# A four-layer graph network on one core: one edge tile a group of layer 3 made on chip by TensorE instead of gathered, and another mix of gathers, single rows and TensorE in layer 2

## The chip, the core and the metric

The kernel runs on one core of a Trainium2 chip. The core has TensorE (PE: matmuls; PEld are its weight loads), VectorE (DVE), ScalarE (ACT), GpSimd (POOL) and SyncE (SP), each with its own queue of instructions. The metric is the device time of one execution in microseconds. The kernel before took 16186.58 us, the median of three runs (16184.84 to 16187.52).

## The reference

There are 12500 nodes with 64 features, 400000 edges sorted by `dst`, an edge type (8 of them) for each edge and a node type (4) for each node. Four layers follow each other, each `x = layernorm(x + layer(x))`. The change touches the third and the fourth, which the kernel and this text count from zero as layers 2 and 3:

```python
# layer 2
msg_sum = segment_sum(feature[src], dst)          # mean over the edges of each node, then
h = where(deg > 0, msg_sum / max(deg, 1), 0)      # a gate of 3 groups and a 64x64 matrix
# layer 3
k, q, v = (typed_linear(x, W, ntype) for W in (Wk, Wq, Wv))   # the matrix is chosen by node type
kw = typed_head_linear(k[src], rel_att, etype)    # 4 heads of 16, the matrix chosen by edge type
m  = typed_head_linear(v[src], rel_msg, etype)
a  = (kw * q[dst]).sum(-1) * rel_pri[:, etype].T / sqrt(16)
alpha = softmax of a over the edges of each dst
h  = segment_sum(m * alpha, dst)                  # then typed_linear(h, Wa, ntype)
```

So layer 2 needs one row of x for each edge, and layer 3 a row of 64 keys and 64 values for each edge, which depends on the source node, its type and the type of the edge.

## The kernel before, in words

**Tiling.** The edges lie in 128 lanes of `EP` = 3125 columns; a column is a tile of 128 edges. Columns are taken in groups of `G` = 25: `groups` (L194) has 124 of these, then 16, 8 and 1 columns, 127 in all. The nodes are 98 tiles of 128 (`NT`), in blocks of `NB` = 7 (`NBA` = 14). Since edges are sorted by `dst`, sums over the edges of a node are scans along a lane, and their ends are picked up later.

**Gathers.** `gather` (L214) is an indirect DMA that POOL issues: 128 rows of a table in device memory, by a column of indices, into one tile of SBUF. Instead of it, `row_by_row` (L234 on) moves single rows by direct DMAs from the queues of SP and ACT, 128 (or half of them) for one tile.

**Layer 2's edges** (L1168 to L1302) loop over the groups. Each tile `gx[:, j]` of a group comes in one of three ways: by `gather` from `X2`; in the groups of `single`, chosen by `ROWS2` (L45: those with g % 5 in (1, 3)), the last two columns by rows, one on SP and one on ACT; and in the groups of `dense` (3 to 123) `PE2` tiles (L46: 2 and 3 by turns) by TensorE. For these, `one_hots_of` spreads the keys by a matmul into `pk` (L1241) and compares them on DVE (L1244) to a one-hot tile `hot`; `products` multiplies it with x, which lies in SBUF as a sum of three bf16 `parts` (39 matmuls, L1257); of the eight nodes that share a key, `take` picks the right one by a mask and a sum on DVE (L1267 to L1270). Then 25 scans on DVE add up the rows along the lanes (L1293). The order on SP, ACT, PE and DVE is that of the program (`manual_schedule`); one-hots are made three groups ahead, products and rows two groups ahead.

**Layer 2's nodes** (`nodes2`) finish x for a block, write it to `xs`, and put into the table `TKM` in device memory keys and values for each node and each of the eight edge types. `in_turn` (L179) interleaves the stages of several blocks, in program order.

**Layer 3's edges** (L1429 to L1558): `step(g, c0, ng)` does one group. POOL gathers its 25 tiles of 128 keys and values from `TKM` (in every third group, `ROWS3`, SP loads one by rows, in two halves). DVE carries the query of each edge along the lane into `st` (25 dependent instructions, L1462), multiplies with the keys and reduces (`pr`, `sc`, five columns at a time, L1469 and L1470), scans the running maximum `M` (L1477) and takes the differences `ex`. ACT exponentiates them twice (`weight`, L1485, into PSUM; `ex`, L1486). DVE scans the sum `L` (L1489), ACT spreads the decay `dec` (L1492), DVE multiplies values by `weight` (`wm`, L1497, four instructions) and scans `hs` (L1502); ACT copies `hs`, `M` and `L` to `R` (L1505 to L1507), which SP writes out. `gk` and `st` have three buffers, so that POOL and the loads run ahead. Here only SP is in program order; the order of the other engines is a scheduler's.

**Layer 3's nodes** (`nodes3`) pick up the ends of the lanes, apply `Wa` by node type, add `xs` and normalize.

Of the kernel before, what the change touches and what calls it, by code (L numbers as in the profile page):

```python
# [19 lines left out]
P = 128  # L20
# [21 lines left out]
WAIT2 = 16  # L42
WAIT3, EVERY3 = 2, 1
ACTN = 3
ROWS2 = 5, (1, 3)  # L45
PE2 = 2, 3  # L46
NC = 13
ROWS3 = 3
RL = 32
# [5 lines left out]
def resnorm_gnn_kernel(ctx: ExitStack, tc: tile.TileContext, a: dict, out: bass.AP):  # L55
# [20 lines left out]
    NBA = NT // NB  # L76

    const = ctx.enter_context(tc.tile_pool(name="const", bufs=1))
    to_l2 = ExitStack()
    to_l0 = ExitStack()  # L80
    right = "right"
# [20 lines left out]
    def lanes(table):  # L102
        return table[:E, :].rearrange("(p c) f -> p c f", p=P)
# [110 lines left out]
    def gather(to, table, at):  # L214
        return nc.gpsimd.indirect_dma_start(  # L215
            out=to, out_offset=None, in_=table, in_offset=bass.IndirectOffsetOnAxis(ap=at, axis=0)
        )
# [168 lines left out]
    xs = const.tile([P, NT, D], F32, name="xs")  # L386
    if NREM:
        nc.vector.memset(xs[:, NFULL:, :], 0.0)
        nc.sync.dma_start(xs[:NREM, NFULL, :], x[NFULL * P :, :])
# [477 lines left out]
        nc.vector.tensor_add(fixS, pos, away)  # L867

    keep = const.tile([P, EP], F32, name="keep")
    negm = const.tile([P, EP], F32, name="negm")  # L870
    w64 = const.tile([D, P], F32, name="w64")
    neg64 = const.tile([D, P], F32, name="neg64")
    fixG = const.tile([P, 1], I32, name="fixG")
# [291 lines left out]
        in_turn(nodes01, [NB] * (NBA - 1) + [4, 2, 1], lambda n: EVERY1)  # L1165
    to_n1.close()


    with tc.tile_pool(name="e2", bufs=2) as sb:
        pm = sb.tile([P, D], F32, name="m2", bufs=1)  # L1170
# [23 lines left out]

        parts = [sb.tile([P, NT, D], BF, name=f"part{k}", bufs=1) for k in range(3)]
        for b in range(NBA):
            t = slice(b * NB, (b + 1) * NB)
            rest = xs[:, t, :]
            for k in range(3):
                nc.scalar.activation(parts[k][:, t, :], rest, AF.Copy)  # L1200
                if k < 2:
                    left = sb.tile([P, NB, D], F32, name=f"left{k}")
                    nc.vector.tensor_sub(left, rest, parts[k][:, t, :])
                    rest = left
# [5 lines left out]

        def by_pe(g):

            return range(G - 2 - PE2[g % 2], G - 2) if g in dense else ()

        keys = sb.tile([P, n], HF, name="keys", bufs=1)
        key_b = sb.tile([P, n], F32, name="key_b", bufs=1)
# [87 lines left out]
        put_ends(R2, row)  # L1304

    to_l2.close()

    def types_of(t, t0, nt):

# [23 lines left out]
    with tc.tile_pool(name="n2", bufs=1) as sb, tc.tile_pool(name="n2ps", bufs=2, space=PSUM) as psp:  # L1333
        puts = []

        def nodes2(b, t0, nt):
# [65 lines left out]
            for j in range(nt):  # L1402

                put = start_row(t0 + j, q[:, j, :])
                tc.declare_no_dep(put.ins, group="starts", reason="distinct rows")
                tc.add_to_no_dep_group("starts", put.ins)
                puts.append(put)
                s = slice(j * P, (j + 1) * P)
                km = sb.tile([P, ETY, 2, D], F32, name=f"km_{j % 4}")
                pws = [psp.tile([P, ETY, D], F32, name="pw", bufs=4) for _ in range(2)]  # L1410
                for w, pw in enumerate(pws):
                    of = slice(w * D, (w + 1) * D)
                    nc.tensor.matmul(pw.rearrange("p e f -> p (e f)"), kv[of, s], wkm[of].rearrange("p e f -> p (e f)"),
                                     start=True, stop=True)
                for w, pw in enumerate(pws):
                    nc.scalar.activation(km[:, :, w, :], pw, AF.Copy)
                r = (t0 + j) * P
                nc.sync.dma_start(
                    TKM[r * ETY : (r + P) * ETY, :].rearrange("(p e) f -> p (e f)", e=ETY),
                    km.rearrange("p e w f -> p (e w f)"),  # L1420
                )
                yield

        in_turn(nodes2, [1, 2, 4] + [NB] * (NBA - 1), lambda n: n + 1,
                {getattr(mybir.EngineType, e) for e in ('PE', 'Activation', 'DVE', 'SP')})


    with tc.tile_pool(name="e3", bufs=2) as sb, tc.tile_pool(name="e3ps", bufs=1, space=PSUM) as psp:
# [26 lines left out]
        def step(g, c0, ng):  # L1455
            nonlocal pa, M, L, hs, last, R
            gk, st = keys_of(g), sts.pop(g)
            for j in range(ng - (g in single)):
                gather(gk[:, j, :], TKM, stS[:, c0 + j : c0 + j + 1])
            for j in range(ng):  # L1460
                c = c0 + j
                nc.vector.scalar_tensor_tensor(st[:, j, :], pa, keep[:, c : c + 1], st[:, j, :],  # L1462
                                               op0=ALU.mult, op1=ALU.add)
                pa = st[:, j, :]
            sc = sb.tile([P, NH, ng], F32, name="sc")
            for q in range(0, ng, 5):
                s = slice(q, min(q + 5, ng))
                pr = sb.tile([P, 5, D], F32, name="pr")[:, : s.stop - q]
                nc.vector.tensor_mul(pr, st[:, s], gk[:, s, :D])  # L1469
                nc.vector.tensor_reduce(sc[:, :, s].rearrange("p h c -> p c h"),  # L1470
                                        pr.rearrange("p c (h d) -> p c h d", d=HS), AX.X, ALU.add)
            nm = negm[:, c0 : c0 + ng]
# [9 lines left out]
            nc.vector.tensor_sub(ex[:, 1, :, 1:], sc, M[:, :, 1:])  # L1482

            weight = psp.tile([P, NH, ng], F32, name="weight", bufs=2)
            nc.scalar.activation(weight, ex[:, 1, :, 1:], AF.Exp)  # L1485
# [27 lines left out]
            for ahead, half in ((3, 0), (2, 1)):  # L1513
                if g + ahead in single:
                    to, k = keys_of(g + ahead)[:, G - 1, :], single.index(g + ahead)
                    for p in range(half * P // 2, (half + 1) * P // 2, RL):
                        row_by_row(TKMb, 8 * D, p, (nc.sync, SP, to, places3[k : k + 1, :]))

        R = None
        with tc.manual_schedule(engines={SP}):  # L1520
            load_starts(0)
            load_starts(1)
            for g, (c0, ng) in enumerate(groups):
                step(g, c0, ng)

        row = ends_of_lanes(sb, R3, W3)

# [41 lines left out]
    with tc.tile_pool(name="n3", bufs=1) as sb, tc.tile_pool(name="n3ps", bufs=2, space=PSUM) as psp:  # L1569
        def nodes3(b, t0, nt):  # L1570
# [69 lines left out]
```

## Time and profile before

| | us |
|---|---|
| median of three runs | 16186.58 |
| profiled execution | 16233.31 |
| its span | 16231.3 |
| layer 2's edges, from the first gather on | 8385 to 11882 |
| layer 2's nodes | 11882 to 12168 |
| layer 3's edges | 12168 to 16074 |
| layer 3's nodes | 16074 to 16231 |

| engine | busy us | share of the span |
|---|---|---|
| PE | 7861.8 | 48% |
| DVE | 10882.3 | 67% |
| ACT | 2682.9 | 17% |
| POOL | 12159.1 | 75% |

The granted PE clock was 0.71 over the span. A row of the profile names the source line, the engine, the operation, the tile that is written and those that are read, the shape and the number of instructions; then their busy time, the mean of one, and how long the engine stood idle just before them and what ended that. A row of waits has the engine, what waited, what it waited for, and the total, number and longest of these waits. "issue" is time in which the engine waited for nothing that the profile shows.

### The profile page before, as it was taken

The page shows a single profiled execution, that of the slowest core. Times are in us where ns is not written, and L with a number is a line of the kernel's source. Part 1 is how long each engine was busy: PE and PEld are TensorE (multiplying, and loading weights), DVE is VectorE, ACT ScalarE, POOL GpSimd, SP SyncE. Part 2 cuts the span into 40 slices and gives each one's busy share as a digit, 9 for nine tenths or more (in the row PEclk, how much of TensorE's full clock was granted, in tenths as well). Part 3 has the DMA queues.
Part 4 walks back from the last instruction along what each step waited for, and adds up shares of the span by engine and source line. Part 5 has one row for each costly group of instructions (what it writes and reads, how often), then busy time and mean ns, then how long its engine had stood idle before and what let it go on. Part 6 is the DMA issues. An engine that isn't in the chain of part 4 may idle for free. (4 is left out here: it accounts for less than half of the span.)

```text
span 16231.3 us, 220160 instructions
## 1 busy us (share of the span) xinstructions
PE 7861.8 (48%) x54548; PEld 5552.5 (34%) x54548; DVE 10882.3 (67%) x29577; ACT 2682.9 (17%) x5002; POOL 12159.1 (75%) x12630
## 2 busy tenths in 40 slices
PE   4454666666663566666547777777760000000002
PEld 4443555555553455555523333333340000000002
DVE  9995777777774577777445555555545666666666
ACT  0012333333332011111020000000031212222222
POOL 7777777777777777777767777777767777777776
PEclk6666777777776787777768888888885555555555
DMA  3333332222221565656312222222253333333333
GB/s 78 120 104 85 87 91 82 72 56 52 53 57 48 169 201 195 204 197 202 111 41 54 59 58 57 55 58 58 58 187 103 110 108 109 113 107 111 109 109 97
DMA packets 1136527, 1634.07 MB, mean 101 GB/s; under 512 B 762674, under 2 KB 768306, under 8 KB 1134850
## 3 DMA queue, kind: packets, MB, share of 16 engines
q1 hardware_dynamic: 693282, 1094.42, 20.1%
q0 software_dynamic: 403872, 517.47, 13.6%
q10 hardware_dynamic: 38080, 8.06, 0.2%
q8 instruction: 432, 7.08, 0.2%
q14 instruction: 861, 7.05, 0.1%
HBM read 881.78 MB, written 737.15 MB: 100 GB/s over the span
## 5 line engine op out<-in xcount | busy, mean ns | idle before, releaser
L780 POOL DMA_INDIRECT SRT<-at,to x3090 | 3011.7, 975 | 943.2 <-issue 909.6
L215 POOL DMA_INDIRECT gk<-TKM,stS x3084 | 2934.3, 951 | 940.9 <-issue 926.3
L215 POOL DMA_INDIRECT gx<-X,srcS x2724 | 2591.8, 951 | 923.2 <-issue 785.3
L1257 PE MATMUL pr<-part,hot 128*128 128x512 bf16 (+1 forms) x11817 | 2549.3, 379 | 504.3 <-DVE one L1269 493.7
L215 POOL DMA_INDIRECT gb<-TB,srcS x2125 | 2079.7, 979 | 648.2 <-issue 629.0
L956 PE MATMUL ps_c<-ident,full 128*64 128x128 f32 x3 | 1.3, 421 | 3908.4 <-DVE full L1529 3906.9
L1293 DVE SCALAR_TENSOR_TENSOR gx<-gx,keep 128x64 f32<-128x64 f32 x3124 | 890.5, 285 | 1457.8 <-DMA gx<-X 1042.6
L1257 PEld LDWEIGHTS <-hot 128*128 128x128 bf16 x11817 | 1154.6, 100 | 1891.8 <-issue 674.2
L1089 DVE SCALAR_TENSOR_TENSOR R<-R,negm,msg 128x64 f32<-128x64 f32 x3124 | 854.3, 273 | 828.2 <-PE msg L1020 823.7
L956 PEld LDWEIGHTS ps_c<-ident,full 128*64 128x64 f32 x3 | 0.4, 128 | 3909.8 <-DVE full L1529 3907.7
L215 POOL DMA_INDIRECT xg<-in_x,srcS x1000 | 956.0, 956 | 306.3 <-issue 297.6
L1469 DVE TENSOR_TENSOR pr<-st,gk 128x320 f32<-128x320 f32 x627 | 306.8, 489 | 1143.6 <-DMA gk<-TKM,stS 1117.7
L1462 DVE SCALAR_TENSOR_TENSOR st<-st,keep 128x64 f32<-128x64 f32 x3124 | 886.3, 284 | 209.0 <-DMA st<-S 114.3
L372 DVE TENSOR_TENSOR ol<-iota,lo 128x512 f16<-128x512 f32 (+2 forms) x1000 | 979.4, 979 | 0.0
L681 PE MATMUL pT<-identh,oh 128*98 128x128 f16 x3125 | 405.0, 259 | 1157.1 <-DVE oh L369 1154.8
L1014 PE MATMUL pt<-ident,st 128*128 128x128 f32 (+1 forms) x3250 | 825.7, 353 | 214.4 <-DVE st L1080 195.8
L729 PE MATMUL pG<-ol,mb 128*128 128x128 f16 x4625 | 774.1, 241 | 184.7 <-ACT mb L713 182.7
L1080 DVE SCALAR_TENSOR_TENSOR st<-st,keep 128x64 f32<-128x64 f32 x3124 | 862.3, 276 | 1.3
L1013 PE MATMUL pt<-ident,gb 128*128 128x128 f32 (+1 forms) x2210 | 574.8, 355 | 591.6 <-DMA gb<-TB,srcS 585.2
L1048 DVE SCALAR_TENSOR_TENSOR r<-r,keep 128x64 f32<-128x64 f32 x3000 | 829.9, 277 | 0.0
L369 DVE TENSOR_TENSOR oh<-iota,hi 128x392 f16<-128x392 f32 (+2 forms) x1000 | 784.6, 785 | 23.6 <-DMA xg<-in_x,srcS 23.6
L1014 PEld LDWEIGHTS pt<-ident,st 128*128 128x128 f32 (+1 forms) x3250 | 630.9, 244 | 289.1 <-DVE st L1080 243.3
(353 smaller groups left out, 19603.5 us busy)
## 6 DMA issues: line engine op xcount, KB each, us to landing
st<-S SPq DMA_DIRECT2D x248, 800.0 KB
R<-R SPq DMA_DIRECT2D x124, 900.0 KB
r<-SRT SPq DMA_DIRECT2D x125, 812.5 KB
R<-r SPq DMA_DIRECT2D x125, 812.5 KB
gx<-X ACTq DMA_DIRECT2D x6272, 0.2 KB
gx<-X SPq DMA_DIRECT2D x6272, 0.2 KB
S<-zero SPq DMA_DIRECT2D x200, 500.0 KB
R<-R SPq DMA_DIRECT2D x124, 800.0 KB
```

The source lines that it names most:

```text
L215: return nc.gpsimd.indirect_dma_start(out=to, out_offset=None, in_=table, in_offset=bass.IndirectOffsetOnAxis(ap=at, axis=0))
L369: nc.vector.tensor_tensor(oh, iota[:, None, :NT].to_broadcast([P, n, NT]), hi[:, :, None].to_broadcast([P, n, NT]), ALU.is_equal)
L372: nc.vector.tensor_tensor(ol, iota[:, None, :].to_broadcast([P, n, P]), lo[:, :, None].to_broadcast([P, n, P]), ALU.is_equal)
L729: nc.tensor.matmul(pG[:, j, :], l, r, start=(n == 0), stop=(n == len(terms) - 1))
L780: put = nc.gpsimd.indirect_dma_start(out=SRT, out_offset=bass.IndirectOffsetOnAxis(ap=to[:, j : j + 1], axis=0), in_=at[:, j, :], in_offse ...
L1014: nc.tensor.matmul(pt[:w, k, :], two_tiles(st, k, w), ident, start=False, stop=True)
L1048: nc.vector.scalar_tensor_tensor(r1[:, j, :D], pm1, keep1[:, c : c + 1], r1[:, j, :D], op0=ALU.mult, op1=ALU.add)
L1080: nc.vector.scalar_tensor_tensor(st[:, j, :], pa, keep[:, c : c + 1], st[:, j, :], op0=ALU.mult, op1=ALU.add)
L1089: nc.vector.scalar_tensor_tensor(R[:, j, :], pm, negm[:, c : c + 1], msg[:, j - q, :], op0=ALU.add, op1=ALU.max)
L1257: nc.tensor.matmul(pr[:, :m, :].rearrange("p b f -> p (b f)"), hot[:, c, :], parts[part][:, 8 * c : 8 * c + m, :].rearrange("p b f -> p (b ...
L1293: nc.vector.scalar_tensor_tensor(gx[:, j, :], pm, keep[:, c : c + 1], gx[:, j, :], op0=ALU.mult, op1=ALU.add)
L1462: nc.vector.scalar_tensor_tensor(st[:, j, :], pa, keep[:, c : c + 1], st[:, j, :], op0=ALU.mult, op1=ALU.add)
```

## The change

In layer 2, `ROWS2` becomes every third group with one residue (40 groups of two row tiles where there were 49), and `PE2` a cycle of 3, 3, 3, 2 (332 tiles by TensorE where there were 303).

In layer 3, in the 121 groups of `dense` (3 to 123), column 22 is no longer gathered. TensorE makes it from x, which `nodes2` now also leaves in SBUF as three bf16 parts `x3`, in stages that stand by hand in the steps of the groups around it. They pick the row of x (one-hot, 39 products, a mask, eight summing matmuls to `x1`) and the type of the node (13 narrow products to `p8`), multiply by the matrices of all types (`keys_and_values`), choose the edge type by a mask and sum 16 matmuls to `kv1`, and ACT puts that into `gk`. The two `weights` tiles, `p8`, `x1` and `kv1` are slices of one tile `bank2` in PSUM; `weight` was a tile of its own before. DVE, PE, ACT and SP now all keep the order of the program in this loop. `nm` is computed for each group instead of read from `negm`, `xs` and `negm` move to other pools, and `nodes3` adds the three parts of `x3` instead of `xs`.

```diff
-ROWS2 = 5, (1, 3)
-PE2 = 2, 3
+ROWS2 = 3, (1,)
+PE2 = 3, 3, 3, 2
...
+            in_parts(lambda shape, name: tile_of(shape, name, 1), xs, x3, cols)
...
+        bank = psp.tile([P, 4 * P], F32, name="bank")
+        pk, tT, kvT = bank[:, :P], bank[:, P : 3 * P], bank[:, 3 * P :]
+        bank2 = psp.tile([P, 4 * P], F32, name="bank2")
+        weights = [bank2[:, k * P : k * P + NH * G].rearrange("p (h c) -> p h c", h=NH) for k in range(2)]
+        p8 = bank2[:, 2 * P : 2 * P + 8]
+        x1, kv1 = bank2[:, 5 * D : 6 * D], bank2[:, 6 * D :]
...
+        def only(rows, hot8):
+            one = sb.tile([P, 8, D], F32, name="one", bufs=3)
+            nc.vector.tensor_mul(one, rows, hot8[:, :, None].to_broadcast([P, 8, D]))
+            return one
+        def sum_of(to, one):
+            for b in range(8):
+                nc.tensor.matmul(to, ident, one[:, b, :], start=(b == 0), stop=(b == 7))
...
+        def products_3(g):
+            hot = hots.pop(g)
+            of_x[g] = pr = psp.tile([P, 8, D], F32, name="big", bufs=2)
...
+            for c in range(NC):
+                m = min(8, NT - 8 * c)
+                nc.tensor.matmul(p8[:, :m], hot[:, c, :], ntab[:, 8 * c : 8 * c + m], start=(c == 0), stop=(c == NC - 1))
+        def take_3(g):
...
+            nc.vector.tensor_scalar(hb, frow[:, :8], key_b[:, 0, k : k + 1], None, op0=ALU.is_equal)
+            sum_of(x1, only(pr, hb))
...
+            nc.vector.tensor_mul(t8, p8, hb)
...
+        def keys_and_values(g):
...
+                pw = psp.tile([P, ETY, D], F32, name="big", bufs=2)
...
+        def choose_3(g):
...
+            chosen[g] = [only(pw, he) for pw in by_edge_type.pop(g)]
+        def sums_3(g):
+            for w, one in enumerate(chosen.pop(g)):
+                sum_of(kv1[:, w * D : (w + 1) * D], one)
+        def put_3(g):
+            nc.scalar.activation(keys_of(g)[:, by_pe, :], kv1, AF.Copy)
...
             for j in range(ng - (g in single)):
+                if g in dense and j == by_pe:
+                    continue
                 gather(gk[:, j, :], TKM, stS[:, c0 + j : c0 + j + 1])
...
                 pa = st[:, j, :]
+            on(g + 1, choose_3)
+            on(g + 3, one_hot_3)
+            on(g + 2, products_3)
+            on(g + 1, sums_3)
             sc = sb.tile([P, NH, ng], F32, name="sc")
...
-            weight = psp.tile([P, NH, ng], F32, name="weight", bufs=2)
+            weight = weights[g % 2][:, :, :ng]
             nc.scalar.activation(weight, ex[:, 1, :, 1:], AF.Exp)
             nc.scalar.activation(ex, ex, AF.Exp)
+            on(g + 3, compare_3)
...
+            on(g + 2, take_3)
             hs = sb.tile([P, D, ng + 1], F32, name="hs")
...
+            on(g + 2, place_3)
             R = sb.tile([P, ng, W3], F32, name="R", bufs=2)
...
+            on(g + 1, put_3)
             nc.sync.dma_start(lanes(R3)[:, c0 : c0 + ng, :], R)
...
-        with tc.manual_schedule(engines={SP}):
+        with tc.manual_schedule(engines={SP, ACT, mybir.EngineType.PE, mybir.EngineType.DVE}):
...
             for g, (c0, ng) in enumerate(groups):
+                on(g + 1, keys_and_values)
                 step(g, c0, ng)
...
-            nc.vector.tensor_add(y, po, xs[:, cols, :])
+            nc.vector.tensor_add(y, x3[0][:, cols, :], x3[1][:, cols, :])
+            nc.vector.tensor_add(y, y, x3[2][:, cols, :])
+            nc.vector.tensor_add(y, y, po)
```

`one_hot_3` and `compare_3` are the two halves of layer 2's `one_hots_of` for one tile. `on(g, ...)` runs the stages for group g if it is one of `dense`.

More of the change, by code (lines that the diff above doesn't have):

```diff
@@ L78, in resnorm_gnn_kernel @@
     const = ctx.enter_context(tc.tile_pool(name="const", bufs=1))
+    to_l3 = ExitStack()
+    xpool = to_l3.enter_context(tc.tile_pool(name="xpool", bufs=1))
     to_l2 = ExitStack()
@@ L384, in row_bcast @@
         return t
-    xs = const.tile([P, NT, D], F32, name="xs")
+    xs = xpool.tile([P, NT, D], F32, name="xs")
     if NREM:
@@ L869, in resnorm_gnn_kernel @@
     keep = const.tile([P, EP], F32, name="keep")
-    negm = const.tile([P, EP], F32, name="negm")
+    negm = edges2.tile([P, EP], F32, name="negm")
     w64 = const.tile([D, P], F32, name="w64")
@@ L1166, in resnorm_gnn_kernel, with in_parts @@
     to_n1.close()
+    def in_parts(tile_of, table, parts, t):
+        rest = table[:, t, :]
+        for k in range(3):
+            nc.scalar.activation(parts[k][:, t, :], rest, AF.Copy)
+            if k < 2:
+                left = tile_of([P, t.stop - t.start, D], f"left{k}")
+                nc.vector.tensor_sub(left, rest, parts[k][:, t, :])
+                rest = left
     with tc.tile_pool(name="e2", bufs=2) as sb:
@@ L1196, in resnorm_gnn_kernel @@
         for b in range(NBA):
[L1197 to L1204, printed above, removed]
+            in_parts(lambda shape, name: sb.tile(shape, F32, name=name), xs, parts, slice(b * NB, (b + 1) * NB))
         own = sb.tile([P, NC], F32, name="own", bufs=1)
@@ L1211, in by_pe @@
         def by_pe(g):
-            return range(G - 2 - PE2[g % 2], G - 2) if g in dense else ()
+            return range(G - 2 - PE2[g % len(PE2)], G - 2) if g in dense else ()
         keys = sb.tile([P, n], HF, name="keys", bufs=1)
@@ L1306, in resnorm_gnn_kernel @@
     to_l2.close()
+    parts3 = ctx.enter_context(tc.tile_pool(name="parts3", bufs=1, side=right))
+    x3 = [parts3.tile([P, NT, D], BF, name=f"x3_{k}") for k in range(3)]
+    ntab = parts3.tile([P, NT], BF, name="ntab")
     def types_of(t, t0, nt):
@@ L1422, in nodes2, with one_hot_3, compare_3, place_3 @@
                 yield
+            in_parts(lambda shape, name: tile_of(shape, name, 1), xs, x3, cols)
         in_turn(nodes2, [1, 2, 4] + [NB] * (NBA - 1), lambda n: n + 1,
                 {getattr(mybir.EngineType, e) for e in ('PE', 'Activation', 'DVE', 'SP')})
-    with tc.tile_pool(name="e3", bufs=2) as sb, tc.tile_pool(name="e3ps", bufs=1, space=PSUM) as psp:
+    to_l3.close()
+    with tc.tile_pool(name="e3", bufs=2) as sb:
+      with (tc.tile_pool(name="e3k", bufs=1) as ksb):
+        types = ksb.tile([P, NT], I32, name="types")
+        nc.vector.memset(types, 0)
+        of = a["node_type_4"]
+        nc.sync.dma_start(types[:, :NFULL], of[: NFULL * P].rearrange("(t p) -> p t", p=P))
+        if NREM:
+            nc.sync.dma_start(types[:NREM, NFULL:], of[NFULL * P :].rearrange("(t p) -> p t", t=1))
+        nc.vector.tensor_copy(ntab, types)
+        dense = range(3, NG - 1)
+        nd = len(dense)
+        by_pe = G - 3
+        keys = sb.tile([P, nd], HF, name="keys", bufs=1)
+        key_b = sb.tile([P, 2, nd], F32, name="key_b", bufs=1)
+        at = groups[dense[0]][0] + by_pe
+        of = stS[:, at : at + (nd - 1) * G + 1 : G]
+        part_i = ksb.tile([P, 4, nd], I32, name="part_i")
+        for k, (by, mask) in enumerate(((13, None), (3, 127), (10, 7), (0, 7))):
+            if by:
+                nc.vector.tensor_scalar(part_i[:, k], of, by, None, op0=ALU.arith_shift_right)
+            if mask:
+                nc.vector.tensor_scalar(part_i[:, k], part_i[:, k] if by else of, mask, None, op0=ALU.bitwise_and)
+        nc.vector.scalar_tensor_tensor(keys, part_i[:, 0], float(P), part_i[:, 1], op0=ALU.mult, op1=ALU.add)
+        nc.vector.tensor_copy(key_b, part_i[:, 2:])
+        own = sb.tile([P, NC], F32, name="own", bufs=1)
+        nc.vector.tensor_scalar(own, frow[:, :NC], float(P), pcol, op0=ALU.mult, op1=ALU.add)
+      with tc.tile_pool(name="e3ps", bufs=1, space=PSUM) as psp:
+        bank = psp.tile([P, 4 * P], F32, name="bank")
[4 more added lines that the diff above has]
+        x1, kv1 = bank2[:, 5 * D : 6 * D], bank2[:, 6 * D :]
+        hots, of_x, by_types, chosen, place_of_type, by_edge_type = {}, {}, {}, {}, {}, {}
+        def only(rows, hot8):
[5 more added lines that the diff above has]
+                nc.tensor.matmul(to, ident, one[:, b, :], start=(b == 0), stop=(b == 7))
+        def one_hot_3(g):
+            k = g - dense[0]
+            nc.tensor.matmul(pk, keys[:, k : k + 1].to_broadcast([P, P]), identh, start=True, stop=True)
+        def compare_3(g):
+            hots[g] = hot = sb.tile([P, NC, P], BF, name="hot", bufs=2)
+            nc.vector.tensor_tensor(hot, pk[:, None, :].to_broadcast([P, NC, P]),
+                                    own[:, :, None].to_broadcast([P, NC, P]), ALU.is_equal)
+        def products_3(g):
[3 more added lines that the diff above has]
+                m = min(8, NT - 8 * c)
+                for part in range(3):
+                    nc.tensor.matmul(pr[:, :m, :].rearrange("p b f -> p (b f)"), hot[:, c, :],
+                                     x3[part][:, 8 * c : 8 * c + m, :].rearrange("p b f -> p (b f)"),
+                                     start=(c == 0 and part == 0), stop=(c == NC - 1 and part == 2))
+            for c in range(NC):
+                m = min(8, NT - 8 * c)
+                nc.tensor.matmul(p8[:, :m], hot[:, c, :], ntab[:, 8 * c : 8 * c + m], start=(c == 0), stop=(c == NC - 1))
+        def take_3(g):
+            k, pr = g - dense[0], of_x.pop(g)
+            hb = sb.tile([P, 8], F32, name="hb")
+            nc.vector.tensor_scalar(hb, frow[:, :8], key_b[:, 0, k : k + 1], None, op0=ALU.is_equal)
+            sum_of(x1, only(pr, hb))
+            place_of_type[g] = ht = sb.tile([P, NTY], F32, name="ht")
+            t8 = sb.tile([P, 8], F32, name="t8")
+            nc.vector.tensor_mul(t8, p8, hb)
+            ty = sb.tile([P, 1], F32, name="ty")
+            nc.vector.tensor_reduce(ty, t8, AX.X, ALU.add)
+            nc.vector.tensor_scalar(ht, frow[:, :NTY], ty, None, op0=ALU.is_equal)
+        def place_3(g):
+            ht = place_of_type.pop(g)
+            by_types[g] = bt = sb.tile([P, NTY, D], F32, name="bt")
+            nc.vector.tensor_mul(bt, x1[:, None, :].to_broadcast([P, NTY, D]), ht[:, :, None].to_broadcast([P, NTY, D]))
+        def keys_and_values(g):
+            bt = by_types.pop(g)
+            for k in range(2):
+                nc.tensor.transpose(tT[:, k * P : (k + 1) * P], bt[:, 2 * k : 2 * k + 2, :].rearrange("p t f -> p (t f)"), ident)
+            tTs = sb.tile([P, 2 * P], F32, name="tTs", bufs=1)
+            nc.scalar.activation(tTs, tT, AF.Copy)
+            for k in range(2):
+                nc.tensor.matmul(kvT, wkqv[:, k, 0:2, :].rearrange("p s f -> p (s f)"), tTs[:, k * P : (k + 1) * P],
+                                 start=(k == 0), stop=(k == 1))
+            kvTs = sb.tile([P, P], F32, name="kvTs", bufs=1)
+            nc.scalar.activation(kvTs, kvT, AF.Copy)
+            by_edge_type[g] = []
+            for w in range(2):
+                of = slice(w * D, (w + 1) * D)
+                pw = psp.tile([P, ETY, D], F32, name="big", bufs=2)
+                nc.tensor.matmul(pw.rearrange("p e f -> p (e f)"), kvTs[of], wkm[of].rearrange("p e f -> p (e f)"),
+                                 start=True, stop=True)
+                by_edge_type[g].append(pw)
+        def choose_3(g):
+            k = g - dense[0]
+            he = sb.tile([P, ETY], F32, name="he")
+            nc.vector.tensor_scalar(he, frow[:, :ETY], key_b[:, 1, k : k + 1], None, op0=ALU.is_equal)
+            chosen[g] = [only(pw, he) for pw in by_edge_type.pop(g)]
[4 more added lines that the diff above has]
+            nc.scalar.activation(keys_of(g)[:, by_pe, :], kv1, AF.Copy)
+        def on(g, *stages):
+            if g in dense:
+                for stage in stages:
+                    stage(g)
@@ L1471, in step @@
                                         pr.rearrange("p c (h d) -> p c h d", d=HS), AX.X, ALU.add)
-            nm = negm[:, c0 : c0 + ng]
+            nm = sb.tile([P, ng], F32, name="nm")
+            nc.vector.tensor_scalar(nm, keep[:, c0 : c0 + ng], -NEG, NEG, op0=ALU.mult, op1=ALU.add)
             Mp, Lp, hp = M, L, hs
@@ L1523, in resnorm_gnn_kernel @@
             for g, (c0, ng) in enumerate(groups):
+                on(g + 1, keys_and_values)
                 step(g, c0, ng)
+      with tc.tile_pool(name="e3pe", bufs=1, space=PSUM) as psp:
         row = ends_of_lanes(sb, R3, W3)
```

## The prediction

> **What bounds the kernel now.** I read the page, then a table of the stages the change touches (their ends taken from the timeline), then the waits and groups of layer 3's edges. The table's columns after the stretch are busy time and instructions of PE, PEld, DVE, ACT and POOL, then the granted PE clock, DMA share and GB/s:
>
> ```profile
> 8385.00:11882.00 3497.00, 2560.87 (x12124) 1167.53 (x12124) 2014.89 (x4402) 20.18 (x39) 2592.75 (x2725) 0.86 0.23 57
> 11882.00:12168.00 286.00, 242.65 (x1166) 149.60 (x1166) 125.72 (x300) 154.32 (x318) 194.65 (x197) 0.95 0.68 235
> 12168.00:16074.00 3906.00, 1.63 (x4) 0.56 (x4) 2509.40 (x6684) 792.24 (x891) 2935.30 (x3085) 0.50 0.36 109
> 16074.00:16232.00 158.00, 114.57 (x492) 104.45 (x492) 97.81 (x234) 38.05 (x96) 98.01 (x100) 0.50 0.37 85
> ```
>
> These are layer 2's edges, layer 2's nodes, layer 3's edges and layer 3's nodes. In layer 3's edges PE does nothing at all (4 matmuls, clock 0.50) and POOL is busy 2935 of 3906 us. The waits (total, times, longest) of that stretch, then of layer 2's edges:
>
> ```profile
> POOL gk L215 <- issue: 926.3, 3036, 0.3
> DVE pr L1469 <- DMA gk<-TKM,stS: 1117.7, 245, 9.3
> ACT weight L1485 <- DVE ex L1482: 0.8, 1, 0.8
> ```
>
> ```profile
> DVE gx L1293 <- DMA gx<-X: 1042.6, 44, 37.1
> POOL gx L215 <- DMA gx<-X: 59.5, 60, 7.6
> POOL gx L215 <- DVE gx L1293: 29.8, 55, 13.3
> ```
>
> In layer 3 POOL waits for nothing but its own 0.30 us after each gather: 0.951 + 0.30 = 1.2535 us a gather, 24.67 gathers a group (25, less one in every third group that SP reads by rows), so 31.0 us a group. DVE waits for POOL's rows; when its input is there it needs 20.2 us a group (14075.0 to 14095.2 in the timeline). In layer 2 POOL is the bound as well, but stalls on the row-by-row tiles of SP and ACT (`gx<-X`): summed over the timeline, its gaps above 0.30 us are 69.6 us.
>
> **Layer 3, what leaves POOL.** One gather in each of 121 groups: 121 x 1.2535 = 151.7 us. POOL then needs 23.67 x 1.2535 = 29.7 us a group. That is the whole gain, and only while nothing else takes over 29.7.
>
> **Layer 3, what is added.** Groups now run as a loop written by hand, so DVE no longer mixes the 25 `st` scans with the products. DVE a group in program order: `st` 7.98, five pairs `pr`/`sc` 4.63, M 0.92, `ex` 0.75, L 0.75, `wm` 3.08, `hs` 3.62 = 21.7. Added, by layer 2's rows for the same shapes: compare 1.88 (L1244), three masks at 0.69 (L1269), two 8-wide tests at 0.25 (L1267), and by the nearest small rows (0.2 to 0.26) `nm` 0.2, t8/ty/ht 0.58, and half a mask, 0.42, for `bt`: 5.7. DVE 27.4 a group, still under 29.7. ACT gets two copies for kv and the put, about 1 us in 29. The question is in what order PE, ACT and DVE wait for each other.
>
> In the changed kernel's instructions as built, `weight` (new L1628) lies in one PSUM bank with p8, x1 and kv1. Its ACT instruction waits for the PE count that is reached by the last matmul of sums_3(g+1); PE runs one_hot, products(g+2), sums in that order, and products' first matmul waits for choose_3's first mask, after the `st` scans. Behind `weight` on ACT stand ex, dec, R, put, and the copies of keys_and_values; on DVE, L (needs ex), wm, take, hs, place and the next group's `st`. Before, `weight` had a tile of its own and waited for DVE alone, 0.8 us in the whole stage. [...] No row of before shows two engines sharing a bank here. By the trace alone `weight` would be free at DVE's `ex`, and the loop would be DVE's 27.4 + about 1.75 for x1 = 29.2, under POOL's 29.7. [...]
>
> **The loop, from the first `st` scan.** The PE prices:
>
> ```profile
> 10007.75 10.73 PE L1257 MATMUL pr<-part,hot 128*128 128x512 bf16 x39 [9.67 <-DVE one L1269]
> 10018.49 16.04 PE L1257 MATMUL pr<-part,hot 128*128 128x512 bf16 x78
> ```
>
> ```profile
> 12060.02 3.24 PE L1396 MATMUL po<-wkqv,tT 128*128 128x64 f32 x28
> ```
>
> ```profile
> 16096.87 6.47 PE L1596 MATMUL po<-wa,tT 128*128 128x64 f32 x28 [0.20 <-DVE tT L1329]
> ```
>
> 39 products take 8.02 us in a running stream (16.04/2) and 10.7 after a pause. The 64-wide f32 matmul takes 0.116 us at granted clock 0.95 and 0.231 at 0.50. [...] In the new loop PE is nearly idle from the sums to the next products, save short bursts, so I take 10.1 for the products (mean of such bursts in layer 2, 9.3 to 10.9); always warm would be 8.1. Types: 13 narrow matmuls, not in the trace; each loads its weights (100 ns, L1257's PEld row), so 1.3 us, between 0.9 and 2.1. Then:
> - `st` 7.98, test 0.25, first mask 0.75: 8.98. Products 10.1: 19.1. Types 1.3: 20.4. Sixteen sums 1.86 and handover 0.2: 22.4. DVE has done sc, M, ex and compare by 18.
> - ACT weight 0.26 and ex 0.38 (L1485, L1486) with gaps 0.15: 23.2. L: 23.95. wm: 27.05. Test and mask of take: 28.0.
> - x1's eight matmuls after 5.6 us of PE idling: 0.93 warm, 1.9 cold; 1.75 taken: 29.75. t8/ty/ht: 30.3. hs: 34.0. bt: 34.4.
>
> So 34.4 us a group where there were 31.0: POOL now waits for DVE's `wm` (a buffer of gk), as its batches stand three groups ahead. Keys_and_values(g+1) on PE and ACT is done about 6.9 us into the loop, before choose needs it at 8.2: nothing.
> Stage: POOL's first 98 gathers and step 2's DVE work, 144; 118 loops of 34.4, 4059; the last three full groups 34.4 + 24.2 + 22 as the added stages run out; the 16-, 8- and 1-column groups 30.5. Together 4314, against 3900 now from the first gather (12172.2) to the end of the last scan (16072.0): **+414**.
>
> **Layer 2.** Gathers 3125 - 80 by rows - 332 by PE = 2713 instead of 2724: -13.8 us. A rows tile takes about 68 us (0.532 us a row), and two came in five groups (139.7 us cycle, where POOL's gathers take 136): this is what POOL stalls on. Now there is one in three groups, 68 under 81, so most of the 69.6 goes; 9 stays. The 29 more PE tiles cost DVE 3.85 each, 112 us, and PE 235: DVE 18.3 and PE 22.5 to 26 a group, under POOL's 27.05. If PE's 26 grew by 2 us, the cover would be gone and each group would cost 1 us more, 121 in all. **-75** (-20 to -85).
>
> **The nodes.** x3's three ACT copies and two DVE subtractions per block stand between gT and q, where ACT idled 2.43 us a block; at L1200's 0.574 and L1203's 0.613 they overrun by 0.7 us: +10 for 14 blocks (0 to 25). The node types come as some 12400 four-byte pieces on SP's queue behind the last loads; the nearest row is q10 (38080 packets, 0.2% of 16 engines, 13.6 ns each): +5 (0 to +40). In layer 3's nodes two more additions per block of 0.57 us lie under 7 gathers of 1.25; the last block shows: +3 (0 to +20). Pools moved, `negm` and `xs`: nothing; they change addresses, and nothing queues for them.
>
> **Sum.** +414 - 75 + 10 + 5 + 3 = +357, made against the profiled execution (16233.3, its span 16231.3), which is 46.7 us (0.3%) above the median; on the median 16186.6 + 357 rounds to **16545**.
>
> **Rivals.**
> - POOL stays the bound. It decides where PE's chain from the first mask to the last sum, which I put at 13.4 us, comes down to DVE's 9 (or the wait is met before `weight` is issued). For it: DVE's 27.4 and POOL's clean 29.7. Against: 39 products alone take 8.0 at the best. -152 - 75 + 18 = -209: **15978**, faster. Break-even is a loop of 31.0, sums ending at 19.0.
> - PE warm throughout: products 8.1, types 0.9, x1 0.93, so the loop is about 31.2 to 32.4. At 32: 118 x 2.4 less than the forecast: **16260**, slower. For it: more work on PE each group. Against: 5 us without PE work before x1, and L1596 at 0.50 with just such gaps.
> - PE colder or longer: types at 2.1, sums at 0.23, products half cold, loop of 37 to 42: **16850 to 17450**. For it: L1596's rate in bursts. Against: sums follow 11 us of unbroken PE work.
> - The gather doesn't leave POOL (the skip does nothing): excluded; column 22's gather is not in the built order.
>
> **How the numbers follow.** The forecast has 0.70, POOL-bound 0.08, warm 0.12, cold 0.10. Its own range, loops of 33.2 to 36.6: 16400 to 16800. Down to 16250 takes most of the warm case, 16820 the edge of the cold one; the POOL-bound case is left out. A measurement of this kernel tells about 0.2% from no change. Faster 0.10 (POOL-bound, and warm with the best of layer 2), same 0.04, slower 0.86.
>
> **What would show it.** Right: ACT idle before `weight` ended by PE's sums, some 5 us a group; DVE idle before L about as long; POOL waiting for `wm`, 4 to 5 us a group; products near 10 us; layer 2's POOL stalls gone and its stage about 75 us shorter. Wrong: POOL's `gk` waits still all "issue", or DVE without a gap ahead of L; then the bank's wait was met in time. If products run in 8 us and x1 in 0.9, the clock held.

## The result and the profile after

The changed kernel takes 16804.5 us (median of four runs, 16775.59 to 16819.11), the kernel before 16185.97: ratio 1.038, 95% interval 1.0367 to 1.0393, slower by 618 us. The forecast was 16545, slower by 358. The profiled execution has a span of 16814.4 us, 583 more than before (the profiled run lies 12 us above its median, that of before 47). From the timelines, first gather to last scan of each edge stage:

| stage | before | after | difference | forecast |
|---|---|---|---|---|
| up to layer 2's first gather | 8385.7 | 8368.0 | -18 | 0 |
| layer 2's edges | 3492.5 | 3404.9 | -88 | -75 |
| layer 2's nodes | 294.0 | 301.3 | +7 | +15 |
| layer 3's edges | 3900 | 4572.6 | +673 | +414 |
| layer 3's nodes, to the end | 159.3 | 167.6 | +8 | +3 |

The stages of the changed kernel, with the columns of the table in the prediction (stretch and length; busy time and instructions of PE, PEld, DVE, ACT and POOL; granted PE clock, DMA share, GB/s):

```profile
8368.00:11785.00 3417.00, 2774.47 (x13284) 1271.74 (x13284) 2137.25 (x4507) 19.12 (x38) 2578.55 (x2716) 0.91 0.20 58
11785.00:12072.00 287.00, 243.41 (x1166) 149.44 (x1166) 143.57 (x332) 176.59 (x366) 194.68 (x196) 0.95 0.72 234
12072.00:16650.00 4578.00, 2653.26 (x13435) 1633.18 (x13435) 3159.57 (x8023) 865.43 (x1254) 2860.57 (x2965) 0.66 0.29 91
16650.00:16815.00 165.00, 113.69 (x493) 104.09 (x493) 114.96 (x267) 38.14 (x97) 101.06 (x100) 0.50 0.33 81
```

In layer 3's edges (third row) no engine is busy for more than 69% of the stage: POOL has less to do than before and is idle 1717 us, and the granted clock is 0.66. So what sets its time is a chain that goes from engine to engine. The waits of that stage (total, times, longest) show where it passes:

```profile
ACT bank L1628 <- PE bank L1484: 2112.8, 121, 18.6
POOL gk L217 <- issue: 1625.9, 2815, 10.9
...
DVE L L1633 <- ACT ex L1629: 727.2, 126, 8.6
...
DVE t L1517 <- PE bank L1484: 463.4, 121, 3.8
```

L1628 is `weight`, written to the PSUM bank; L1484 is the summing matmul. ACT waits for the sums in all 121 groups; DVE waits behind that for L, 5.8 us a group, and then 3.8 us a group for the sums of x1. POOL's waits, which were 0.3 us each before, are now up to 10.9; the profile puts nearly all of them down to "issue", but POOL's idle time above 0.3 us a gather is 1683 - 2963 x 0.3 = 794 us, 6.6 a group. One loop in the timeline, DVE (start, duration, line):

```profile
14521.00 7.98 DVE L1600 SCALAR_TENSOR_TENSOR st<-st,keep 128x64 f32<-128x64 f32 x25
...
14536.90 1.88 DVE L1492 TENSOR_TENSOR hot<-bank,own 128x1664 bf16<-128x1664 f32 x1
14545.37 0.76 DVE L1633 TENSOR_TENSOR_SCAN L<-ex,L 128x25 f32<-128x25 f32 x4 [6.59 <-ACT ex L1629]
14546.04 3.02 DVE L1641 TENSOR_TENSOR wm<-gk,bank 128x400 f32<-128x400 f32 x4
...
14553.76 0.17 DVE L1517 TENSOR_TENSOR t<-bank,hb 128x8 f32<-128x8 f32 x1 [3.83 <-PE bank L1484]
...
14558.15 8.04 DVE L1600 SCALAR_TENSOR_TENSOR st<-st,keep 128x64 f32<-128x64 f32 x25
```

and PE, ACT and POOL in the same loop:

```profile
14529.97 10.69 PE L1502 MATMUL big<-x,hot 128*128 128x512 bf16 x39 [1.03 <-DVE one L1479]
14540.50 0.47 PE L1507 MATMUL bank<-ntab,hot 128*128 128x8 bf16 x13
14540.83 3.76 PE L1484 MATMUL bank<-one,ident 128*128 128x64 f32 x32
14550.08 3.65 PE L1484 MATMUL bank<-one,ident 128*128 128x64 f32 x16 [5.49 <-DVE one L1479]
```

```profile
14544.67 0.26 ACT L1628 ACTIVATE bank<-ex 128x100 f32<-128x100 f32 x1 [18.09 <-PE bank L1484]
```

```profile
14549.83 0.94 POOL L217 DMA_INDIRECT gk<-TKM,stS  x1 [8.16 <-issue]
```

DVE has everything for `weight` at 14537.0; the sums end at 14544.6, and `weight` starts at 14544.67. From one `st` to the next the loop takes 37.15 us; the mean of 119 such loops is 36.56, with 34.5 where the products take 8.1 us and 37.1 to 37.7 where they take 10.6 to 11.1. POOL's gather starts 0.77 us after `wm` has ended. In 118 of POOL's 121 waits over 1 us it is between 0.757 and 0.774 us after the end of a `wm`, and the waits come a group (23 or 24 gathers) apart. So they are waits for `wm`, after which a buffer of `gk` is free for the next group, whatever the profile calls them.

### The profile page after: what moved, and what is told of

Its sections match the earlier page's. It is cut to its first block, busy times and chain, and to the rows that moved or that the text cites. A ratio compares the mean times of both kernels' runs of the same rounds, so it can differ in the third digit from the quotient of the medians.

```text
span 16814.4 us, 247584 instructions
## 1 busy us (share of the span) xinstructions
PE 10715.9 (64%) x69139; PEld 7275.6 (43%) x69139; DVE 11694.2 (70%) x31096; ACT 2777.4 (17%) x5413; POOL 12057.6 (72%) x12498
## 5 line engine op out<-in xcount | busy, mean ns | idle before, releaser
L217 POOL DMA_INDIRECT gk<-TKM,stS x2963 | 2859.2, 965 | 1683.4 <-issue 1625.9
L1262 PE MATMUL pr<-part,hot 128*128 128x512 bf16 (+1 forms) x12948 | 2771.6, 376 | 539.1 <-DVE one L1274 521.8
L1262 PEld LDWEIGHTS <-hot 128*128 128x128 bf16 x12948 | 1257.6, 100 | 2040.2 <-issue 690.5
L1484 PE MATMUL bank<-one,ident 128*128 128x64 f32 x5808 | 900.1, 326 | 713.5 <-DVE one L1479 713.5
L1502 PE MATMUL big<-x,hot 128*128 128x512 bf16 (+1 forms) x4719 | 1222.4, 428 | 125.4 <-DVE one L1479 125.4
L1484 PEld LDWEIGHTS bank<-one,ident 128*128 128x128 f32 x5808 | 866.8, 239 | 728.1 <-issue 725.3
L1502 PEld LDWEIGHTS <-hot 128*128 128x128 bf16 x4719 | 517.2, 111 | 882.8 <-issue 506.9
L683 PEld LDWEIGHTS <-oh 128*98 128x98 f16 x3125 | 287.8, 150 | 1242.7 <-DVE oh L371 1238.5
```

The source lines that it names most:

```text
L217: return nc.gpsimd.indirect_dma_start(out=to, out_offset=None, in_=table, in_offset=bass.IndirectOffsetOnAxis(ap=at, axis=0))
L1262: nc.tensor.matmul(pr[:, :m, :].rearrange("p b f -> p (b f)"), hot[:, c, :], parts[part][:, 8 * c : 8 * c + m, :].rearrange("p b f -> p (b ...
L1484: nc.tensor.matmul(to, ident, one[:, b, :], start=(b == 0), stop=(b == 7))
L1502: nc.tensor.matmul(pr[:, :m, :].rearrange("p b f -> p (b f)"), hot[:, c, :], x3[part][:, 8 * c : 8 * c + m, :].rearrange("p b f -> p (b f) ...
```

## Experiments

The theory (A): `weight`, in one bank with p8, x1 and kv1, waits for PE's chain of products and sums, and a second PE wait, x1's, stands in series behind it. Rivals: (B) the order by hand makes DVE slow by itself; (C) another PE wait takes the place of one that is removed; later, what holds up POOL.

Four runs first took layer 2 and the order apart, on one chip on which the kernel before takes 16228.76 us.

**Layer 2's two edits alone**, on the kernel before:

```diff
-ROWS2 = 5, (1, 3)
-PE2 = 2, 3
+ROWS2 = 3, (1,)
+PE2 = 3, 3, 3, 2
...
-            return range(G - 2 - PE2[g % 2], G - 2) if g in dense else ()
+            return range(G - 2 - PE2[g % len(PE2)], G - 2) if g in dense else ()
```

> The kernel before with layer 2's two edits alone (a third of the groups with rows, three tiles by TensorE in three groups of four); layer 3 untouched. Theory A (the changed kernel's layer 2 edges took 92 us less in its profile, and none of that has to do with layer 3): 16186 - 92 = 16094, within 15. Rival (part of it is a shift of layer 1's end or of the layer's start, 17 us): 16110 to 16130.

Measured 16149.77: -79 us, ratio 0.9954 (0.9937 to 0.997). From the start of the first gather to that of the last it is 3406 us instead of 3487. The stage in the changed kernel's profile fell by 88; the 9 us between are not explained.

**Rows alone** (the change to `ROWS2`):

> The kernel before with the rows of layer 2 alone changed: 40 groups with two row tiles instead of 49, every third; TensorE keeps 2 and 3 tiles. 18 gathers more, 18 x 1.2535 = +22.6 us. Theory A (POOL's stalls of 69.6 us come from the queues that move rows, two tiles of 68 us in 136 us of gathers): the stalls go, -60 or so, in sum -35 to -45: 16145. Rival G (the stalls come from DVE or PE): they stay, +23: 16209.

Measured 16188.2: -40.6, ratio 0.9976 (0.9966 to 0.9985), though POOL has 18 gathers more. In the waits of its layer 2, POOL's waits of up to 7.6 us for rows are gone:

```profile
POOL gx L215 <- DMA gx<-X: 3.4, 11, 0.3
```

**Tiles by TensorE alone** (the rest of that diff):

> The kernel before with the tiles by TensorE of layer 2 alone changed: 332 instead of 303, rows as before. 29 gathers fewer, -36 us at 1.2535. Theory A (row queues bound the stage: ACT moves two tiles in 139.7 us in a cycle of five groups, whatever POOL does): POOL stalls instead, gain 0 to 12: 16180. Rival G (POOL's number of gathers alone counts): -36: 16150.

Measured 16228.18: -0.6, ratio 1.0001 (0.9991 to 1.001). 29 gathers fewer bring nothing while the row queues set the pace; POOL only stands longer before the rows (59.5 us before):

```profile
POOL gx L215 <- DMA gx<-X: 90.5, 60, 7.3
```

So the two edits don't add up: -41 and -1 alone, -79 together. The rows had to go first. POOL's idle time above 0.30 us a gather in this stage closes the account: 65 us in the kernel before, 101 with the tiles alone, none with the rows alone or with both. Rows: -65 + 18 x 1.25 = -42. Tiles: +36 - 29 x 1.25 = 0. Both: -65 - 11 x 1.25 = -79.

**The order by hand alone** in layer 3, without the new stages:

```diff
-        with tc.manual_schedule(engines={SP}):
+        with tc.manual_schedule(engines={SP, ACT, mybir.EngineType.PE, mybir.EngineType.DVE}):
             load_starts(0)
```

> The kernel before with one edit: PE, DVE and ACT keep the order of the program in layer 3's loop too, as in the changed kernel. DVE then needs about 21.7 us a group instead of 20.2, since scans and products no longer alternate, against POOL's 31.0. Theory A (the order costs nothing while POOL is the bound; only the end of the loop is a few us longer): 16186 to 16196. Rival B (the order by hand is what slows the loop): 16300 or more.

Measured 16243.58: +14.8, ratio 1.0008 (0.9999 to 1.0018), not told from no change. Rival B has fallen for the loop without the new stages.

**Four edits of the changed kernel** were then meant to take the bank and x1 apart: weight in SBUF (e1, and again e9), t8/ty/ht behind `hs` (e2), both (e3, e10), and matmuls that fill PE's idle time (e4). `type_3` is the part of `take_3` that makes t8, ty and ht.

```diff
-        weights = [bank2[:, k * P : k * P + NH * G].rearrange("p (h c) -> p h c", h=NH) for k in range(2)]
...
-            weight = weights[g % 2][:, :, :ng]
+            weight = sb.tile([P, NH, ng], F32, name="weight", bufs=2)
```

```diff
+        def type_3(g):
...
             on(g + 2, take_3)
             hs = sb.tile([P, D, ng + 1], F32, name="hs")
...
-            on(g + 2, place_3)
+            on(g + 2, type_3, place_3)
```

```diff
+        def fill(n):
+            for _ in range(n):
+                nc.tensor.matmul(kvT, identh, identh, start=True, stop=True)
...
             on(g + 3, compare_3)
+            if g + 2 in dense:
+                fill(70)
...
             on(g + 2, take_3)
+            if g + 2 in dense:
+                fill(50)
```

> The changed kernel, but weight lies in SBUF instead of in the PSUM bank of kv1, p8 and x1; nothing else is touched. Theory A (the shared bank puts PE's chain of products and sums in front of ACT's weight): weight follows DVE's ex at once, about 16.7 us into the loop, L at 18.2, the mask of take at 22.8, x1 runs behind the sums at 23.6, now warm (1.9 us), and the loop ends at 30.0 to 30.5 instead of 36.5. That takes 121 x 6.2 = 750 us from 16804: 16055, within 40, and DVE's 727 us of waiting ahead of L are gone. Rival B (the order by hand makes DVE slow by itself, and PE's lateness is hidden): the loop stays over 35 us, 16700 or more. Rival C (another PE wait, x1's or the products', takes the place): 33 to 35 us, 16400 to 16600.

> The changed kernel, but the three small DVE instructions on the type of the node (t8, ty, ht), which wait for x1's last matmul, stand behind the scan hs instead of ahead of it; the shared bank stays. Theory A (two PE chains in series on the loop's path, the second of them x1's eight matmuls, 3.65 us): hs covers x1, the loop falls from 36.5 to about 33.0, 121 x 3.5 = 425 us: 16380, within 60. Rival C (x1 is late only because all of PE's work is late, so that its wait moves on to the next place): less than 100 us, 16700 or more.

> Both edits at once: weight in SBUF, and t8, ty and ht behind hs. Theory A: DVE's own work, 27.5 us, is all that is left of the loop, which is under POOL's 23.67 gathers at 1.2535 = 29.7; POOL is the bound again with nothing but issue gaps of 0.3, layer 3's edges take some 3770 us instead of 3900 before the change, and with layer 2's gain of about 90 the time is about 15980 (15940 to 16040), faster than both kernels. Rival B (order by hand is slow): over 16400. Rival D (DVE, PE and the gathers get in each other's way in SBUF, so that the gathers take longer): gathers of 1.0 us and more, 16100 or more.

> The changed kernel with matmuls of the identity that nobody reads, 70 behind the sums and 50 behind x1 in each loop, in a PSUM region that is free then, where PE otherwise idles; they come after weight in the order of the program, so weight doesn't wait for them. Theory E (the clock that PE loses in its idle stretches sets x1's 3.65 us and the products' 10.1): x1 takes 1.9, the products 8.1, so the loop is 36.5 - 1.8 - 2.0 = 32.7 and the time 16350, within 60, granted clock of the stage over 0.9. Rival F (these times are the instructions' own and not the clock's): no change, 16800, or longer if the additional matmuls are in the way.

> The changed kernel, but weight lies in SBUF instead of in the PSUM bank of kv1, p8 and x1; nothing else is touched (the kernel of e1, again). Theory A (the shared bank puts PE's chain of products and sums in front of ACT's weight): weight follows DVE's ex at once, L starts about 18 us into the loop, and the loop ends at 30.0 to 30.5 us instead of 36.5: 16804 - 750 = 16055, within 40, and DVE's 727 us of waiting ahead of L are gone. Rival B (the order by hand makes DVE slow by itself): the loop stays over 35 us, 16700 or more. Rival C (another PE wait, x1's or the products', takes the place): 33 to 35 us, 16400 to 16600.

> weight in SBUF, and t8, ty and ht behind the scan hs, which then covers x1's matmuls (the kernel of e3, again). Theory A: DVE's own work, 27.5 us, is all that is left of the loop, under POOL's 23.67 gathers at 1.2535 = 29.7; POOL is the bound again, layer 3's edges take some 3770 us instead of 3900 before the change, and with layer 2's 79 us the time is about 15990 (15950 to 16050), faster than both kernels. Rival B (order by hand is slow): over 16400. Rival D (DVE, PE and the gathers get in each other's way in SBUF, so that a gather takes 1.0 us or more): 16100 or more.

These six runs came on two chips on which the kernel before itself takes 25.8 ms (25832 and 25804 us): there all engines stop again and again, which the profile puts down to "issue" or to no known releaser (in e1 up to 110.4 us on DVE, 56.9 on ACT, 38.9 on PE, and 30.6 before a gather of layer 3). The cause stays open. They took 25232, 25197, 25247, 26428, 25191 and 25212 us in this order; all the numbers of time expected were missed, and the totals say nothing about the question. What can be read is a stretch that holds both PE waits, from DVE's first `ex` to the end of `bt`. Medians: 22.0 us in the changed kernel, 15.3 with weight in SBUF (e1, e9; nearly all loops between 15.3 and 15.4), 12.1 with both edits (e3, e10); with late types alone (e2) it is about 12 in a third of the loops and mostly 17 to 22 in the others, which leaves that edit's worth open. By these medians the bank costs 6.7 us a loop and x1 another 3.2; the stops around the stretch make these rough. In e4 x1 took 1.95 to 3.2 us, 2.5 in the mean, where it takes 3.65 in every loop of the changed kernel (first the usual sums, then x1):

```profile
23003.70 3.76 PE L1484 MATMUL bank<-one,ident 128*128 128x64 f32 x32
...
23013.03 1.97 PE L1484 MATMUL bank<-one,ident 128*128 128x64 f32 x16 [1.65 <-DVE one L1479]
```

The granted clock during x1 is 0.50 in all 121 loops of the changed kernel. In e4 it goes with the time of x1: 1.00 where x1 takes 1.95, 0.62 at 3.0, 0.57 at 3.2. So x1's time goes with the granted clock, as theory E had it. The clock of the whole stage was not brought over 0.9, though (0.70), and what a clock of 1.00 throughout would do to the whole time stays open.

**Weight in SBUF, again**, on a chip on which the kernel before takes 16206.87 us:

> The changed kernel with weight in SBUF (the kernel of e1 and e9, on another chip). [...] Theory A (shared bank): without that disturbance the loop is 15.15 (end of bt to ex, as in the changed kernel) + 15.3 = 30.4 us or a little less where x1 is warm, against 36.56: 16804 - 121 x 6.2 = 16055, within 40. Rival B (the order by hand is slow by itself): loop over 35 us, 16700 or more. Rival C (another PE wait takes the place): 16400 to 16600.

The 15.3 us are the median above, and the disturbance is the stops on the two chips. Measured 16107.07: ratio 0.9939 (0.9923 to 0.9956), 100 us faster than the kernel before and some 700 faster than the changed one, whose ratio was 1.038. Theory A holds, rivals B and C fall; the time is 52 us above the forecast, more than its margin of 40. Waits of layer 3's edges, then the gathers' row, here and in the kernel before:

```profile
ACT weight L1627 <- DVE ex L1624: 1442.9, 125, 47.2
...
POOL gk L217 <- issue: 867.6, 2844, 0.7
...
DVE t L1516 <- PE bank L1483: 350.7, 119, 4.1
...
DVE L L1632 <- ACT ex L1628: 4.3, 7, 0.8
```

```profile
L217 POOL DMA_INDIRECT gk<-TKM,stS x2963 | 2940.4, 992 | 903.9 <-issue 867.6 <-DVE st L1599 13.7 <-DMA gk<-TKM,stS 9.1
```

```profile
L215 POOL DMA_INDIRECT gk<-TKM,stS x3084 | 2934.3, 951 | 940.9 <-issue 926.3 <-DMA gk<-TKM,stS 12.5 <-DMA gk<-TKM 1.8
```

DVE's wait ahead of L fell from 727 to 4 us, and POOL waits for nothing beyond the 0.3 behind each gather (0.7 at the most): POOL is the bound. But its gathers take 0.992 us instead of 0.951, and 23.67 x (0.992 + 0.305) = 30.7 is the loop measured, 30.73. The timeline shows when: POOL, then DVE, in one loop.

```profile
14500.75 0.94 POOL L217 DMA_INDIRECT gk<-TKM,stS  x1 [0.30 <-issue]
14502.00 1.42 POOL L217 DMA_INDIRECT gk<-TKM,stS  x1 [0.30 <-issue]
14503.73 1.18 POOL L217 DMA_INDIRECT gk<-TKM,stS  x1 [0.30 <-issue]
14505.21 0.94 POOL L217 DMA_INDIRECT gk<-TKM,stS  x1 [0.30 <-issue]
```

```profile
14501.12 3.01 DVE L1640 TENSOR_TENSOR wm<-gk,weight 128x400 f32<-128x400 f32 x4
```

Over the stage, 351 gathers that overlap `wm` take 1.231 us in the mean, the other 2612 take 0.960; in the kernel before, where `weight` is in PSUM, it is 0.953 and 0.951. `wm` now has both its inputs in SBUF. Of the 257 gathers over 1.15 us, 198 overlap `wm`; the other 59 overlap `pr`, the product of `st` and `gk`, whose inputs both lie in SBUF as well. The kernel before has 30 gathers over 1.15 us, all of them over `pr`.

**Weight back in PSUM, away from `bank2`.** `dec` writes 1664 columns; in a tile of 2048 (`decs`) two tiles of 100 fit behind it; t8, ty and ht stand behind `hs`:

```diff
-        weights = [bank2[:, k * P : k * P + NH * G].rearrange("p (h c) -> p h c", h=NH) for k in range(2)]
+        decs = psp.tile([P, 16 * P], F32, name="dec")
+        ndec = NH * HS * (G + 1)
+        weights = [decs[:, ndec + k * P : ndec + k * P + NH * G].rearrange("p (h c) -> p h c", h=NH) for k in range(2)]
...
-            dec = psp.tile([P, NH, HS, ng + 1], F32, name="dec")
+            dec = decs[:, : NH * HS * (ng + 1)].rearrange("p (h d c) -> p h d c", h=NH, d=HS)
...
-            on(g + 2, place_3)
+            on(g + 2, type_3, place_3)
```

> The changed kernel with weight in the part of dec's fourth PSUM bank that dec leaves free (no PE output there), and t8, ty and ht behind hs. It differs from the last run in two points: wm reads weight from PSUM again, and x1's matmuls lie under hs. In e11 the loop was 30.72 us: POOL never waited, but its gathers took 0.992 us on average, the longest while wm read both its inputs from SBUF; 23.67 x (0.992 + 0.305) = 30.7. Theory H (two SBUF inputs of wm hold up POOL's gathers): with weight in PSUM no gather is long under wm, the mean is 0.955 to 0.965 as in the changed kernel, the loop is 23.67 x 1.262 = 29.9, and the time is 16107 - 121 x 0.85 = 16005, within 40. Rival I (the gathers are longer because the loop is denser, whatever wm reads): mean 0.99 and more, 16090 to 16120. Rival J (DVE is the bound at its 30 us): ruled out here if POOL again has gaps of 0.30 alone.

Measured 16015.96, 11 us above the forecast, against 16207.43 for the kernel before: ratio 0.9883 (0.9866 to 0.9899), -191 us, faster than both kernels and than layer 2's part alone.

```profile
L217 POOL DMA_INDIRECT gk<-TKM,stS x2963 | 2841.3, 959 | 906.7 <-issue 873.2 <-DVE pr L1617 13.1 <-DMA gk<-TKM 9.8
```

```profile
DVE t L1523 <- PE bank L1486: 9.8, 41, 0.2
...
DVE L L1639 <- ACT ex L1635: 4.5, 7, 0.8
```

435 gathers overlap `wm`, at 0.946 us in the mean, none over 0.98: theory H holds, I falls. What is left of long gathers, 82 over 1.15 us, all overlap `pr`. POOL, then DVE:

```profile
13114.15 1.21 POOL L217 DMA_INDIRECT gk<-TKM,stS  x1 [0.30 <-issue]
```

```profile
13114.06 0.48 DVE L1617 TENSOR_TENSOR pr<-st,gk 128x320 f32<-128x320 f32 x1
```

Both PE waits are gone from DVE, and the stretch from `ex` to the end of `bt`, here without the stops of those two chips, has a median of 11.8 us (14.7 in the run before this one, 22.0 in the changed kernel). Layer 3 goes at POOL's pace again, 23.67 x 1.2645 = 29.9 us a loop (first to last gather 3746.8 us; 3873.9 before, 4541.2 in the changed kernel). Stage by stage this profile is 219 us shorter than that of the kernel before, which was taken on another chip: 92 in layer 2's edges, 121 in layer 3's, 20 ahead of layer 2's first gather, less 14 in the nodes. The late types were not run alone on a chip like this, so their part isn't measured; with POOL the bound in e11 already, the gathers' 0.033 us x 2963 = 98 us are as much as the 91 between the two runs.

## Why the prediction was right, and where its sizes were off

**The mechanism held.** The prediction said that `weight` would wait for the last matmul of sums_3, that DVE would stand ahead of L about 5 us a group, and that the loop would outgrow POOL's 31.0. Measured: 2112.8 us of ACT's waits on L1484 in 121 groups, 5.8 us ahead of L, a loop of 36.56. That `weight` waits for the sums at all, which no row of before shows, it took from the built program, and this decided the sign: with weight in another tile of PSUM (and the late types) the same stages run in 29.9 us, which the prediction had for that case as POOL's 29.7. One thing stays open: `bank2` is one tile as well as one bank, and both were left together, so no run here tells which of the two the wait in the built program guards.

**The size was off by two terms.** Layer 3 got +673, not +414; 121 x (36.56 - 34.4) = 261 is the whole of that. The forecast had sixteen sums in 1.86 us and x1's eight in 1.75; they take 3.76 and 3.65. The row that priced them says x28 for 14 matmuls of the source (7 tiles times 2): such a 128x64 f32 matmul is two instructions in the profile, so 0.116 us was the price of half a matmul. The sums' row above shows it: x32 for 16 matmuls, x16 for 8. At the right count the terms would have been 3.7 and, cold, 3.7. Against that, the 13 type products took 0.47 us instead of 1.3, since their weight loads (0.096 us each) start only 0.025 us apart, and they begin while the products still run. So the sums end 3.93 us behind the products, where types, sums and handover had been put at 3.36, and x1 takes 1.9 more than its 1.75; the steps behind are some 0.3 shorter, since instructions start before the one ahead of them on their engine has ended (`hs` 0.2 us before the end of `ht` in the loop above). 34.4 + 0.6 + 1.9 - 0.3 = 36.6. That the halved price of the sums shows as 0.6 and not as 1.9 is luck: the types had been put too high. With that luck the loop is at the upper edge of the forecast's own range of loops (33.2 to 36.6), and the time 4.5 us above its 16800, inside the wider range to 16820.

**The clock term was right.** Products 10.1 us forecast, 10.1 measured in the mean. It is a mean of two kinds of loops, though: 24 with 8.1 us at a granted clock of 1.00 and 75 with 10.6 to 11.1 at 0.73 to 0.76, the rest between. x1 cold was right too: 0.50 in every loop, and the same 16 instructions take 1.97 where e4 had kept PE busy. What sets the clock, the runs don't settle: PE stands idle 5.5 us before nearly every x1, at 0.50, but 1.65 before x1 in e4, at 1.00 as well as at 0.6, and some 1.0 us before the products at 1.00 as before those at 0.73.

**POOL's wait** was expected on `wm` by name, 4 to 5 us a group. It is 6.6, and the profile calls it "issue" in all but one case; that it is `wm` shows in the 0.76 us by which these gathers follow the end of `wm`.

**Layer 2** gave -79 alone against -75 forecast, and the split shows that the reason was the right one: the rows' queues. The cover on PE and DVE held: POOL has no gap over 0.3 us in that stage of the changed kernel. **Nodes:** +7 and +8 against +15 and +3, within their bounds. The remaining -18 before layer 2's first gather does not follow the edits: that gather also starts at 8364.2 in e7, with a part of layer 2's edits, and at 8386.4 in e5, with all of them.

**The rivals.** "PE warm throughout" (16260) did not happen, though the products ran at a clock of 1.00 in 24 loops; "PE colder or longer" was priced for loops of 37 to 42 and is nearer to what came, for another reason than the one it named. "POOL stays the bound" (15978) is near what the same stages do with weight in a tile without PE's outputs and with late types: 16016.

## What to carry to other kernels

When a change puts a new PE output into a PSUM tile that another engine uses, look up what the waits of that engine's instruction become: here a slice of 100 columns beside PE's outputs cost at least 5.8 us in each of 121 groups (loops of 36.56 us against 30.73 with it in SBUF, where POOL is the bound again), and moving it, with a late use of x1, turned a loss of 618 us into a gain of 191. Before pricing a matmul by a row, divide the row's count by the calls in the source. And where two queues feed one stage (here rows and gathers), relieve the one that is waited for first: the other edit alone gave nothing, and on top of it 38 us.

## What the runs showed of the hardware that was not expected

- POOL's gathers took longer while DVE multiplied with both inputs in SBUF, in the two products of this loop. Gathers over `wm` take 1.231 us in the mean (others 0.960) when both of its inputs are in SBUF (e11), and 0.946 when one is in PSUM (e12). Gathers over `pr`, whose inputs are always both in SBUF, take 1.021 in the last run, and those over neither 0.948.
- With nothing changed from loop to loop, the granted clock differs: in parts of the stage the products take 8.1 us in one loop (clock 1.00) and 10.7 in the next (0.73 to 0.76), and the loops 34.5 and 37.1.
- On two chips the kernel before took 25.8 ms instead of 16.2. The gathers of layer 3 in the edited kernels profiled there took 0.95 to 0.97 us (0.951 in the kernel before on another chip), with stops of all engines between instructions (up to 110.4 us, on DVE in e1). The cause stays open.
